# Centering the last sequence's output on ScalarE, and finishing the last group in two halves

## The chip, the cores and the metric

One core of one Trainium2 chip runs the whole program. The metric is the device time of one execution in microseconds (us). Each core has five engines with their own instruction queues: TensorE (PE in the profile, its weight loads PEld), VectorE (DVE), ScalarE (ACT), GpSimd (POOL) and SyncE (SP), which here issues most transfers. Instructions of different engines run side by side and wait for each other through semaphores; within one engine they start in the order in which they were issued.

## The reference

The input is x, 4 sequences of 2048 tokens with 256 features in float32. The reference applies two layers, each with a residual and a layer norm without gain:

```python
x = layernorm(x + attn(x))       # attn: q, k, v from small MLPs with gelu; scores = tril(q k^T) / scale;
                                 # out = layernorm(scores v) * ln_w + ln_b   (no softmax)
x = layernorm(x + ffn(x))        # ffn: soft mixture of experts over 256 slots (16 experts x 16)
```

In the second layer, tokens are normalized and compared with 256 slot vectors. One softmax (over tokens' logits for a slot) makes the slots' inputs, each expert's MLP turns them into slot outputs `so`, and a second softmax (over the slots, for a token) combines these into the token's output. The kernel's last step for a token is then `layernorm(row + combine @ so)`: the mean and variance over 256 features, the inverse root, and (value - mean) * root.

## The kernel before

The tokens are cut into 16 groups of 512 (W), four per sequence (NG); a group is four chunks (G) of 128 tokens, one token per partition. A group's tokens lie in a buffer `row`, 128 partitions x 4 chunks x 257 values. Eight such buffers exist.

The order of the work is not written out by hand. Functions such as `attend`, `norms`, `back`, `softmaxes`, `slots` and `finish` declare steps with `plan.step(engine, length, emit, reads, writes)`, and `plan.run` is a list scheduler: it repeatedly takes the step that can begin earliest by the given lengths, with ties by rank, and emits its instructions. So a changed length, engine or dependence can move other steps on each engine's queue, and buffers with several places are given out in that order.

`finish(t, so)` ends group t. For each chunk c, TensorE multiplies the combining weights `ct` by the slot outputs `so_t` into a PSUM bank (`ps_at`, three banks; L1265). The product, scaled by a per-token factor `sc`, is added to `row` in one of two ways:

- on VectorE, one instruction from PSUM (L1289);
- in the last sequence (`part` is set), for chunks 1 and 3: ScalarE scales the product from PSUM into a buffer `xn` (L1274), and POOL adds that to `row` (L1281).

`means` then takes VectorE's statistics of the chunk (L532) and their mean and variance (L533) into `mv`. When all four chunks are there, VectorE forms variance + eps (`ve`, L1299), POOL raises it to the power -0.5 (`inv_root`, L521), and `center_on` centers the chunks: first VectorE computes nm = -mean * root for the group (L557), which a ScalarE centering takes as its bias. Then each chunk is centered on the engine that a list names: ScalarE (`Identity` with scale and bias, L567), or VectorE or POOL (`tensor_scalar` with two operations, L573). The list is this:

```python
["ACT"] * G if part is None else
("DVE", "ACT", "POOL", "DVE") if t == ngroups - 1 else ("ACT", "POOL") * 2,
```

SyncE stores the group (L1313), the last group (15) in two halves of two chunks, all others in one transfer of 512 KB.

The finish steps of the sequence before the last (groups 8 to 11) are ranked late (`late = 100`), so they come near the end, just ahead of groups 12 to 15. As built, the eight stores at the end are those of groups 8, 9, 10, 12, 11, 13, 14 and the two halves of 15.

Of the kernel before, what the change touches and what calls it, by code (L numbers as in the profile page):

```python
# [9 lines left out]
AF = mybir.ActivationFunctionType  # L10
ALU = mybir.AluOpType
# [3 lines left out]
P = 128  # L15
G = 4
LAST = 2
W = G * P
LN_EPS = 1e-5
# [164 lines left out]
def _act(n, pointers=0):  # L184
    return 0.16 + 0.00083 * n + 0.093 * pointers
# [6 lines left out]
def _pool(n):  # L192
    return 0.1 + 0.0022 * n


def _pe(n):
    return max(0.22, 0.00168 * n)
# [6 lines left out]
def kernel(  # L204
# [13 lines left out]
    nc = tc.nc  # L218
    B, T, C = x.shape
# [4 lines left out]
    EH = ES // P  # L224
# [11 lines left out]
    ngroups = B * NG  # L236
    plan = Plan()
# [165 lines left out]
    for n, after in (  # L403
# [29 lines left out]
        out=mask,  # L433
        in_=ones,
# [13 lines left out]
    so_t = const.tile([P, EH, C], F32, name="so")  # L448
# [53 lines left out]
    def turn_in(bounce, dst):  # L502
        def emit():
            for a in range(P // 32):
                rows_ = slice(32 * a, 32 * (a + 1))
                nc.sync.dma_start(
                    out=dst[rows_].rearrange("c k (n r) -> c k n r", r=32),
                    in_=bounce[:, :, rows_].rearrange("k (n c) r -> c k n r", c=32),
                )

        plan.step("SP", 2.2, emit, [bounce], [dst])
        plan.step(
            "DVE", _dve(KC * W), lambda: nc.vector.transpose(out=dst.place, in_=dst.place),
            [], [dst],
        )

    def inv_root(v, n):
        r = plan.buffer("root")

        def emit():  # L520
            nc.gpsimd.tensor_tensor(  # L521
                r[:, :n], v[:, :n], nhalf.to_broadcast([P, n]), ALU.pow
            )

        plan.step("POOL", 1.04, emit, [v], [r])
        return r

    def means(src, st, mv, c, access):


        def emit():
            nc.vector.bn_stats(st[:, c, :], access())  # L532
            nc.vector.bn_aggr(mv[:, c, :], st[:, c, :])  # L533

        plan.step("DVE", 0.6, emit, [src], [(st, [c]), (mv, [c])])

    def variances(mv):
        return mv[:, :, 1:2].rearrange("p c o -> p (c o)")
# [10 lines left out]

            plan.step("DVE", 0.42, emit, [mv, r], [(dst, [c])])  # L550

    def center_on(dst, mv, r, engines):

        nm = plan.buffer("root")
        plan.step(
            "DVE", 0.17,
            lambda: nc.vector.scalar_tensor_tensor(  # L557
                nm.place, mv[:, :, 0:1].rearrange("p c o -> p (c o)"), -1.0, r.place,
                ALU.mult, ALU.mult,
            ),  # L560
            [mv, r], [nm],
        )
        for c in range(G):

            def emit(c=c):
                if engines[c] == "ACT":
                    nc.scalar.activation(  # L567
                        dst[:, c, :C], dst[:, c, :C], AF.Identity,
                        bias=nm[:, c : c + 1], scale=r[:, c : c + 1],
                    )  # L570
                else:
                    eng = nc.vector if engines[c] == "DVE" else nc.gpsimd
                    eng.tensor_scalar(  # L573
                        dst[:, c, :C], dst[:, c, :C], mv[:, c, 0:1], r[:, c : c + 1],
                        ALU.subtract, ALU.mult,
                    )

            length = {"ACT": _act(C, 2), "DVE": 0.42, "POOL": _pool(C)}[engines[c]]
            plan.step(
                engines[c], length, emit, [nm if engines[c] == "ACT" else mv, r], [(dst, [c])]  # L580
            )

    def spread(col, name):
# [317 lines left out]
    def norms(t):  # L901
# [17 lines left out]
        for c in range(G):  # L919
# [16 lines left out]
        )  # L936
        rr = inv_root(w2, G)
        center_on(row, mv2, rr, ("DVE", "ACT") * 2)
        plan.step(
            "DVE", 0.17,  # L940
# [139 lines left out]
    def by_blocks(t):  # L1080

        return t < ngroups - LAST
# [164 lines left out]
    def finish(t, so):  # L1247

        b, g = divmod(t, NG)
        row, _, sq, sc = n_tiles.pop(t)
        ct = c_tiles.pop(t)
        if by_blocks(t):
            bounce, ct = ct, plan.buffer("ct", EH)
            turn_in(bounce, ct)
        st, mv = plan.buffer("st", G), plan.buffer("mv", G)

        part = plan.buffer("xn", G) if t >= ngroups - NG else None
        for c in range(G):  # L1260
            pc = plan.buffer("ps_at")

            def emit(c=c, pc=pc):
                for h in range(EH):
                    nc.tensor.matmul(  # L1265
                        pc[:, :C], ct[:, h, c * P : (c + 1) * P], so_t[:, h, :],
                        start=(h == 0), stop=(h == EH - 1),
                    )

            plan.step("PE", EH * _pe(C), emit, [ct, so], [pc])  # L1270
            if part and c % 2:

                def emit(c=c, pc=pc):
                    nc.scalar.activation(  # L1274
                        part[:, c, :], pc[:, :C], AF.Copy, scale=sc[:, c : c + 1]
                    )

                plan.step("ACT", _act(C, 1), emit, [pc, sc], [(part, [c])])

                def emit(c=c):  # L1280
                    nc.gpsimd.tensor_tensor(  # L1281
                        row[:, c, :C], row[:, c, :C], part[:, c, :], ALU.add
                    )

                plan.step("POOL", _pool(C), emit, [(part, [c])], [(row, [c])])
            else:

                def emit(c=c, pc=pc):
                    nc.vector.scalar_tensor_tensor(  # L1289
                        row[:, c, :C], pc[:, :C], sc[:, c : c + 1], row[:, c, :C],  # L1290
                        ALU.mult, ALU.add,
                    )

                plan.step("DVE", 0.48, emit, [pc, sc], [(row, [c])])
            means((row, [c]), st, mv, c, lambda c=c: row[:, c, :C])
        ve = plan.buffer("ve")

        def emit():
            nc.vector.scalar_tensor_tensor(  # L1299
                ve.place, sq.place, LN_EPS, variances(mv), ALU.mult, ALU.add  # L1300
            )

        plan.step("DVE", 0.17, emit, [mv, sq], [ve])
        center_on(
            row, mv, inv_root(ve, G),
            ["ACT"] * G if part is None else
            ("DVE", "ACT", "POOL", "DVE") if t == ngroups - 1 else ("ACT", "POOL") * 2,
        )
        for c0 in range(0, G, G // 2) if t == ngroups - 1 else (0,):
            cs = slice(c0, c0 + (G // 2 if t == ngroups - 1 else G))  # L1310

            def emit(cs=cs):
                nc.sync.dma_start(  # L1313
                    out=out[b, g * W + cs.start * P : g * W + cs.stop * P, :].rearrange(
                        "(c p) d -> p c d", p=P
                    ),
                    in_=row[:, cs, :C],
                )

            plan.step("SP", 0.5, emit, [(row, list(range(cs.start, cs.stop)))], [])  # L1320


    plan.begin(-2.0)
# [8 lines left out]
    for t in range(ngroups):  # L1332
        plan.begin(t)
        attend(t)
        plan.begin(t + 0.7)
        norms(t)
        plan.begin(t + 0.8)
        load_x(t + 2)
        plan.begin(t + 1.2)
        back(t)  # L1340
        if t % NG == NG - 1:
            b = t // NG
            plan.begin(t + 1.5)
            softmaxes(b)


            late = 100.0 if b == B - 2 else 0.0
            plan.begin(t + 1.8 + late)
            so = slots(b)
            for i in range(NG):  # L1350
                plan.begin(t + 2.2 + 0.3 * i + late)
                finish(t - NG + 1 + i, so)
# [44 lines left out]
```

## Time and profile before

| | |
|---|---|
| Time, median of 3 runs | 691.25 us (691.01 to 691.26) |
| The profiled execution's own time | 689.66 us |
| Its span | 687.9 us, granted TensorE clock 0.993 |
| Busy in the span: PE, DVE, ACT, POOL | 660.1, 510.6, 252.3, 261.8 us |
| POOL centerings (L573) | 7, mean 1248 ns |
| ScalarE centerings (L567) | 87, mean 591 ns |
| VectorE centerings (L573) | 34, mean 411 ns |
| Roots on POOL (L521, 128x4) | 48, mean 1019 ns |
| Last matmuls of the program (L1265) | 660.83 to 674.91 us |
| Issues of the last five stores | 674.27, 676.42, 681.98, 683.80, 684.43 us |

The span is the time between the first and last instruction that the hardware profiler saw; the time of an execution also has what lies around it, 1.8 us in the profiled one. "x48 | 48.9, 1019" in a row of groups means 48 instructions that were busy for 48.9 us in total, 1019 ns each; what follows is idle time of the engine just before them and what ended it. Busy shares average over the whole program. At the end, when TensorE has stopped, other engines set the time, so the last 25 us are read by themselves.

### The profile page before, as it was taken

How to read it: one execution, taken by the hardware profiler on the slowest of the kernel's cores; microseconds unless marked ns; L12 is line 12 of the kernel's file. 1: busy time of each engine (PE TensorE's matmuls, PEld its weight loads, DVE VectorE, ACT ScalarE, POOL GpSimd, SP SyncE). 2: the span in 40 equal slices, each digit the busy share in tenths (PEclk: the TensorE clock that was granted, in tenths of full speed). 3: DMA queues.
4: the chain of work that ended last, by engine and by line, in shares of the span. 5: the costliest groups of instructions: out<-in, count | busy, mean ns of one | idle time of the engine just before them, and what ended most of it. 6: DMA issues, size and time to landing. Idle time of an engine off the chain costs nothing.

```text
span 687.9 us, 9055 instructions
## 1 busy us (share of the span) xinstructions
PE 660.1 (96%) x2974; PEld 502.9 (73%) x2974; DVE 510.6 (74%) x1316; ACT 252.3 (37%) x521; POOL 261.8 (38%) x255
## 2 busy tenths in 40 slices
PE   6999999999999999899999999999999999998982
PEld 4758767686868877768677886868676877877871
DVE  1438877968887588968797489998796897768394
ACT  3120335234154226241526125541526444415253
POOL 4260440232346017241418213543415545045247
PEclk9999999999999999999999999999999999999997
DMA  8793177556645146685655364775574316100044
GB/s 244 190 215 63 38 148 143 103 92 122 123 86 98 45 78 186 156 162 103 129 93 92 62 115 130 161 177 117 98 137 79 61 31 92 31 1 1 31 93 152
DMA packets 302462, 73.61 MB, mean 107 GB/s; under 512 B 240016, under 2 KB 302224, under 8 KB 302416
## 3 DMA queue, kind: packets, MB, share of 16 engines
q1 hardware_dynamic: 301312, 71.98, 50.0%
q10 hardware_dynamic: 960, 0.80, 0.4%
q8 instruction: 23, 0.38, 0.2%
q0 software_dynamic: 144, 0.26, 0.1%
q14 instruction: 23, 0.19, 0.1%
HBM read 42.61 MB, written 30.41 MB: 106 GB/s over the span
## 4 chain that ended last, share of the span: by engine, by line
PE 80%; DVE 9%; POOL 4%; DMA 3%; issue 1%; SPq 1%; ACT 1%; POOLq 0%; ACTq 0%; DVEq 0%
PE mm L714 21%; PE mm L1020 7%; PE mm L764 7%; PE at L816 7%; PE at L1142 6%; PE mm L737 6%; PE at L1265 6%; PE at L851 6%; PE at L789 4%; PE at L855 3%; PE at L859 3%; DVE st L532 2%; DMA both_sb<-in_W2q_dram 1%; DVE a_t L892 1%; POOL row L573 1%; POOL root L521 1%
## 5 line engine op out<-in xcount | busy, mean ns | idle before, releaser
L724 ACT ACTIVATE hid<-mm,cols_sb 128x512 f32<-128x512 f32 x96 | 65.1, 685 | 186.9 <-PE mm L714 173.9
L521 POOL TENSOR_TENSOR root<-ve,nhalf 128x4 f32<-128x4 f32 x48 | 48.9, 1019 | 202.0 <-DVE ve L915 76.8
L567 ACT ACTIVATE row<-row,root,root 128x256 f32<-128x256 f32 x87 | 46.5, 591 | 68.6 <-DVE root L557 68.4
L851 PE MATMUL at<-state,hid 128*128 128x256 f32 x240 | 61.8, 380 | 0.0
L737 PE MATMUL mm<-both_sb,hid 128*128 128x257 f32 x256 | 60.8, 381 | 0.9 <-DVE kt L747 0.7
L764 PE MATMUL mm<-W2v_sb,hid 128*128 128x256 f32 x256 | 59.0, 380 | 2.5 <-DVE lg L1030 2.0
L714 PE MATMUL mm<-xT,W1q_sb 128*128 128x512 f32 x128 | 60.7, 604 | 0.3 <-DVE xT L455 0.3
L1053 ACT ACTIVATE xn<-lg,nrm 128x256 f32<-128x256 f32 x64 | 32.0, 500 | 76.4 <-DVE lg L1030 76.3
L1265 PE MATMUL at<-so,ct 128*128 128x256 f32 x256 | 57.9, 380 | 1.8 <-DVE so L1242 1.8
L816 PE MATMUL at<-vt,kt 128*128 128x256 f32 x240 | 58.9, 379 | 0.0
L714 PE MATMUL mm<-xT,W1v_sb 128*128 128x512 f32 x128 | 58.5, 592 | 0.0
L1020 PE MATMUL mm<-mu_sb,xnT 128*128 128x256 f32 x256 | 58.1, 379 | 0.2 <-DVE kt L747 0.2
L714 PE MATMUL mm<-xT,W1k_sb 128*128 128x512 f32 x128 | 58.2, 592 | 0.0
L1142 PE MATMUL at<-row,lg 128*128 128x257 f32 x256 | 56.9, 380 | 0.0
L532 DVE BATCH_NORM_STATS2 st<-row 128x6 f32<-128x256 f32 x128 | 53.6, 419 | 4.0 <-POOL row L1281 1.9
L737 PEld LDWEIGHTS mm<-both_sb,hid 128*128 128x128 f32 x256 | 47.7, 190 | 12.0 <-issue 3.5
L764 PEld LDWEIGHTS mm<-W2v_sb,hid 128*128 128x128 f32 x256 | 48.2, 190 | 10.1 <-DVE lg L1030 2.4
L1265 PEld LDWEIGHTS at<-so,ct 128*128 128x128 f32 x256 | 48.1, 190 | 9.7 <-DVE so L1242 2.2
L1020 PEld LDWEIGHTS mm<-mu_sb,xnT 128*128 128x128 f32 x256 | 48.3, 190 | 8.7 <-issue 1.2
L1142 PEld LDWEIGHTS at<-row,lg 128*128 128x128 f32 x256 | 48.4, 189 | 7.4 <-issue 0.3
L851 PEld LDWEIGHTS at<-state,hid 128*128 128x128 f32 x240 | 45.4, 190 | 9.2 <-issue 2.6
L816 PEld LDWEIGHTS at<-vt,kt 128*128 128x128 f32 x240 | 45.3, 190 | 8.1 <-issue 1.2
(126 smaller groups left out, 1160.5 us busy)
## 6 DMA issues: line engine op xcount, KB each, us to landing
bounce<-xn SPq DMA_DIRECT2D x28, 512.0 KB, 3.2
row<-in_x_dram SPq DMA_DIRECT2D x16, 512.0 KB, 5.2
out_dram<-row SPq DMA_DIRECT2D x15, 512.0 KB, 2.9
xT<-in_x_dram SPq DMA_DIRECT2D x112, 64.0 KB, 2.4
bounce<-kt SPq DMA_DIRECT2D x28, 256.0 KB, 2.8
kT<-bounce SPq DMA_DIRECT2D x56, 128.0 KB, 2.9
xnT<-bounce SPq DMA_DIRECT2D x56, 128.0 KB, 3.6
ct<-bounce SPq DMA_DIRECT2D x56, 128.0 KB, 3.6
```

Source lines behind the costliest of these rows:

```text
L521: nc.gpsimd.tensor_tensor(r[:, :n], v[:, :n], nhalf.to_broadcast([P, n]), ALU.pow)
L532: nc.vector.bn_stats(st[:, c, :], access())
L567: nc.scalar.activation(dst[:, c, :C], dst[:, c, :C], AF.Identity, bias=nm[:, c : c + 1], scale=r[:, c : c + 1],)
L714: nc.tensor.matmul(ph.place, wa[f"W1{n}"][:, k, m * P : (m + 1) * P], xT[:, k, :], start=(k == 0), stop=(k == KC - 1),)
L724: nc.scalar.activation(hid[n][:, m, :], ph.place, AF.Gelu, bias=cols_sb[:, 4 * i + m : 4 * i + m + 1],)
L737: nc.tensor.matmul(pk[:, : C + 1], hid["k"][:, k, c * P : (c + 1) * P], wqk_sb[:, k, :], start=(k == 0), stop=(k == KC - 1),)
L764: nc.tensor.matmul(pv[:, j * C : (j + 1) * C], hid["v"][:, k, (c0 + j) * P : (c0 + j + 1) * P], wa["W2v"][:, k, :], start=(k == 0), stop=( ...
L816: nc.tensor.matmul(pds[:, m * C : (m + 1) * C], kt[:, c, m * P : (m + 1) * P], vt[:, c, :], start=True, stop=True,)
L851: nc.tensor.matmul(po[:, :C], qT[:, k, toks[c]], s[:, k, :], start=(k == 0), stop=False,)
L1020: nc.tensor.matmul(pl[:, j * ES : (j + 1) * ES], xnT[:, k, (c0 + j) * P : (c0 + j + 1) * P], mu_sb[:, k, :], start=(k == 0), stop=(k == KC ...
L1142: nc.tensor.matmul(psi[:, : C + 1], lg[:, c, h * P : (h + 1) * P], row[:, c, :], start=(i == 0 and c == 0), stop=(i == NG - 1 and c == G - 1),
L1265: nc.tensor.matmul(pc[:, :C], ct[:, h, c * P : (c + 1) * P], so_t[:, h, :], start=(h == 0), stop=(h == EH - 1),)
```

## The change

`center_on` gets a first chunk `c0` and a list of engines, one for each chunk from there on; it knows only ScalarE and VectorE. In `finish`, groups 12 to 14 now have all four chunks centered by ScalarE. Group 15 runs the whole ending (evict, statistics, variance, root, nm, centering, store) for chunks 0 and 1, and then for chunks 2 and 3, with the first of each pair centered by VectorE and the second by ScalarE. In group 15 the chunks that go through ScalarE and POOL's addition are now 0 and 2, not 1 and 3. The code for one chunk's product has moved into a function `combine`. The planner's length for a ScalarE centering is 0.55 in place of `_act(C, 2)`, which is 0.56.

```diff
-    def center_on(dst, mv, r, engines):
+    def center_on(dst, mv, r, engines, c0=0):
+        n = len(engines)
         nm = plan.buffer("root")
         plan.step(
             "DVE", 0.17,
             lambda: nc.vector.scalar_tensor_tensor(
-                nm.place, mv[:, :, 0:1].rearrange("p c o -> p (c o)"), -1.0, r.place,
-                ALU.mult, ALU.mult,
+                nm[:, :n], mv[:, c0 : c0 + n, 0:1].rearrange("p c o -> p (c o)"), -1.0,
+                r[:, :n], ALU.mult, ALU.mult,
             ),
-            [mv, r], [nm],
+            [(mv, list(range(c0, c0 + n))), r], [nm],
         )
-        for c in range(G):
+        for i, engine in enumerate(engines):
+            c = c0 + i
...
-                    eng = nc.vector if engines[c] == "DVE" else nc.gpsimd
-                    eng.tensor_scalar(
-                        dst[:, c, :C], dst[:, c, :C], mv[:, c, 0:1], r[:, c : c + 1],
+                    nc.vector.tensor_scalar(
+                        dst[:, c, :C], dst[:, c, :C], mv[:, c, 0:1], r[:, i : i + 1],
                         ALU.subtract, ALU.mult,
                     )
...
         part = plan.buffer("xn", G) if t >= ngroups - NG else None
-        for c in range(G):
-            pc = plan.buffer("ps_at")
...
-            if part and c % 2:
...
-        center_on(
-            row, mv, inv_root(ve, G),
-            ["ACT"] * G if part is None else
-            ("DVE", "ACT", "POOL", "DVE") if t == ngroups - 1 else ("ACT", "POOL") * 2,
-        )
-        for c0 in range(0, G, G // 2) if t == ngroups - 1 else (0,):
...
+        last = t == ngroups - 1
+        n = G // 2 if last else G
+        for c0 in range(0, G, n):
+            cs = list(range(c0, c0 + n))
+            for c in cs:
+                combine(c, row, ct, so, sc, part if part and (c + last) % 2 else None)
+                means((row, [c]), st, mv, c, lambda c=c: row[:, c, :C])
+            ve = plan.buffer("ve")
+            def emit(c0=c0, ve=ve):
+                nc.vector.scalar_tensor_tensor(
+                    ve[:, :n], sq[:, c0 : c0 + n], LN_EPS, variances(mv)[:, c0 : c0 + n],
+                    ALU.mult, ALU.add,
+                )
+            plan.step("DVE", 0.17, emit, [(mv, cs), sq], [ve])
+            center_on(row, mv, inv_root(ve, n), ("DVE", "ACT") if last else ("ACT",) * G, c0)
+            def emit(c0=c0):
+                nc.sync.dma_start(
+                    out=out[b, g * W + c0 * P : g * W + (c0 + n) * P, :].rearrange(
+                        "(c p) d -> p c d", p=P
+                    ),
+                    in_=row[:, c0 : c0 + n, :C],
+                )
+            plan.step("SP", 0.5, emit, [(row, cs)], [])
+
+    def combine(c, row, ct, so, sc, part):
+        pc = plan.buffer("ps_at")
...
+        plan.step("PE", EH * _pe(C), emit, [ct, so], [pc])
+        if part:
...
+                lambda: nc.scalar.activation(
+                    part[:, c, :], pc[:, :C], AF.Copy, scale=sc[:, c : c + 1]
+                ),
...
+                lambda: nc.gpsimd.tensor_tensor(
+                    row[:, c, :C], row[:, c, :C], part[:, c, :], ALU.add
+                ),
...
+            return
...
+            lambda: nc.vector.scalar_tensor_tensor(
+                row[:, c, :C], pc[:, :C], sc[:, c : c + 1], row[:, c, :C],
+                ALU.mult, ALU.add,
+            ),
```

## The prediction

> **What bounds it now.** I read the page first, then a table by stretch, then the chain that ended last. TensorE is busy for 96% of the span, so only what delays TensorE, or what comes after its last matmul, can move the end.
>
> ```profile
> span 687.9 us, 9055 instructions
> PE 660.1 (96%) x2974; PEld 502.9 (73%) x2974; DVE 510.6 (74%) x1316; ACT 252.3 (37%) x521; POOL 261.8 (38%) x255
> ```
>
> The built orders of the two kernels agree on TensorE in every row. On the other engines they part only after POOL's root of group 12, which starts at 667.68 us. So the change lives in the last 20 us. A table of stretches (busy us and count per engine, then clock, DMA share, GB/s):
>
> ```profile
> 676.30:682.00 5.70, 0.00 (x0) 0.00 (x0) 2.43 (x9) 1.09 (x2) 5.49 (x8) 0.73 0.33 114
> 682.00:687.90 5.90, 0.00 (x0) 0.00 (x0) 0.89 (x3) 0.60 (x1) 2.29 (x2) 0.50 0.51 178
> 682.90:684.40 1.50, 0.00 (x0) 0.00 (x0) 0.89 (x3) 0.60 (x1) 1.40 (x2) 0.50 0.94 339
> 684.70:686.20 1.50, 0.00 (x0) 0.00 (x0) 0.00 (x0) 0.00 (x0) 0.00 (x0) 0.50 0.99 336
> ```
>
> After TensorE's end (674.9) POOL is busy 5.49 of 5.70 us and ScalarE 1.09: POOL is the engine of the tail. In the last two rows DMA engines are 94 and 99% busy: a store in flight fills them, at 336 to 339 GB/s. The chain that ended last, in order of time (start, us, what):
>
> ```profile
> 667.68 1.03 POOL root L521
> 668.81 2.44 POOL row L573 x2
> ...
> 672.81 1.04 POOL root L521
> 673.94 2.46 POOL row L573 x2
> 676.40 0.61 POOL row L1281
> ...
> 678.37 1.04 POOL root L521
> 679.50 2.45 POOL row L573 x2
> 681.95 0.99 POOL root L521
> 682.99 1.42 POOLq L1390
> ```
>
> POOL's centerings (L573) are on the chain in three groups, and group 15's root at 681.95 waits behind group 14's centering. Its own input was ready at 679.57. Meanwhile ScalarE, which holds the other centerings, stands still before group 14 and again before group 15:
>
> ```profile
> 675.38 0.59 ACT L567 ACTIVATE row<-row,root,root 128x256 f32<-128x256 f32 x1
> 679.67 1.09 ACT L567 ACTIVATE row<-row,root,root 128x256 f32<-128x256 f32 x2 [3.71 <-DVE root L557]
> 683.17 0.60 ACT L567 ACTIVATE row<-row,root,root 128x256 f32<-128x256 f32 x1 [2.41 <-DVE root L557]
> ```
>
> The last POOL centering ends at 684.40. The last store is issued at 684.43 and lands 2.3 us later at 686.7; closing the program takes the span to 687.9, 1.15 more. Prices, grouped by form (count, then total us, mean ns):
>
> ```profile
> L521 POOL TENSOR_TENSOR root<-ve,nhalf 128x4 f32<-128x4 f32 x48 | 48.9, 1019 | 202.0 <-DVE ve L915 76.8 <-DVE ve L941 56.7 <-DVE ve L1299 43.4
> L567 ACT ACTIVATE row<-row,root,root 128x256 f32<-128x256 f32 x87 | 46.5, 591 | 68.6 <-DVE root L557 68.4
> L573 DVE TENSOR_SCALAR row<-row,mv,root 128x256 f32<-128x256 f32 x34 | 12.7, 411 | 0.0
> L573 POOL TENSOR_SCALAR row<-row,mv,root 128x256 f32<-128x256 f32 x7 | 8.7, 1248 | 0.4
> L521 POOL TENSOR_TENSOR root<-cm,nhalf 128x2 f32<-128x2 f32 x1 | 0.7, 723 | 8.9 <-DVE nscale L626 8.9
> ```
>
> The stores from 660 us on:
>
> ```profile
> DMA to landing us min/median/max: 2.2/2.9/3.0
> ```
>
> **What the Trainium skill says.** "ScalarE: Activation LUTs", section "What ACT_TABLE_LOAD costs", prices an ACTIVATE with a pointer bias at 280 ns + 0.833 per element, 93 more for a second pointer, and lets neighbours overlap by 93. For 256 elements that is 586 ns, and 493 from start to start. The trace agrees: 591 ns, and the four centerings of group 10 start at 661.21, 661.71, 662.20, 662.70. "SBUF — State Buffer", "Who interferes with whom", says that VectorE instructions with two SBUF inputs contend with GpSimd's reads, and that ScalarE waits on nobody at those ports. The trace agrees: the variance step L1299 took 581 ns at 677.71 beside POOL's additions, 164 at 679.40. "DMA: Bandwidth & Descriptors", "Issuing engines are not separate DMA queues", says all transfers share the same 16 engines; the 0.99 share above agrees.
>
> **The change, part by part.** Removed: seven POOL centerings, 7 x 1.25 = 8.7 us (two each in groups 12 to 14, one in 15). Added: seven ScalarE centerings, 7 x 0.49 = 3.45 us of its queue. Group 15 gets a second variance step and a second nm step (L557) on VectorE, about 0.16 us each, and two roots of 128x2 (723 ns, the one row of that shape) in place of one of 128x4: 1.45 against 1.02. Group 15's chunks trade evictors: 0 and 2 now go through ScalarE and POOL's addition, 1 and 3 through VectorE. VectorE's two centerings stay in number, and so do the stores.
>
> Now the order as built, with the starts of before as long as nothing moved. ScalarE: eviction of group 14's chunk 1 at 669.83; three centerings of group 12 from 670.20; eviction at 671.67 (as before, TensorE paces it); fourth centering 672.03; eviction of group 15's chunk 0 at 672.52 (its matmul ends 672.32). At 672.89 one centering of group 11, at 673.38 one of group 13. The eviction of chunk 2 follows its matmul (674.05), at 674.09. Then three of group 13 from 674.46 (an eviction holds the queue 0.37), three of group 11 from 675.93, and the queue is free for group 14 at 677.41.
>
> Does anything feed it late? POOL first: add of group 13 at 668.70, add of group 14's chunk 1 at 670.38 to 671.06, root of group 13 at 671.34 to 672.36, so its nm is there by 672.55, 0.8 before ScalarE asks. Group 11's nm is now queued behind four statistics pairs on VectorE, at 672.32 to 672.45 against 670.17 before; ScalarE asks at 672.89, so this delay costs nothing, with 0.44 in hand. VectorE then: eviction of group 15's chunk 1 at 673.22 (0.48); statistics of it and of group 14's last chunk at about 0.56 a pair, to 674.94; group 14's variance step at 674.97, which POOL's addition (674.64 to 675.30) holds to 675.30. POOL's root of group 14: 675.38 to 676.40. VectorE goes on: chunk 3's eviction 675.22, statistics, variance of the first half at 676.3, two more pairs, and only then group 14's nm at 677.48 to 677.61, though its root was ready at 676.40. So ScalarE waits 0.24 and starts group 14 at 677.65: four centerings, ended at 679.73. First half of group 15 at 679.62, second at 680.12, ended at 680.72. The half roots (676.5 to 677.25, 677.8 to 678.6) are 1.5 us or more ahead of that: splitting the root is hidden behind group 14's centerings on ScalarE; without that cover it would cost its 0.43.
>
> So compute ends at 680.7 rather than 684.4: 3.7 gained. But the stores bunch. Group 13 goes out at 676.1, group 11 at 677.5; each fills the DMA engines for 512 KB / 338 GB/s = 1.55 us. Group 14's store is issued at 679.76, and the halves at 680.25 and 680.76. Group 14 alone lands 2.9 later, at 682.66; the 512 KB of both halves queue behind it for 1.55 more: 684.2. Without the queue the last half would land at 680.76 + 2.3 = 683.1. Before, group 14 was issued 1.8 and 2.45 us ahead of the halves, and its data was out of the way; this is where 1.1 of the 3.7 goes. Closing adds 1.15: span 685.4, that is 2.5 less. The profiled execution took 689.66 and would take 687.2; the runs' median is 1.59 above it, and I carry the same 2.5 over: 691.25 - 2.5 = 688.75. About 0.2%, 1.4 us, is what a measurement can tell from no change.
>
> **Unknowns.** The 128x2 root on this data is bounded by 0.72 and 1.02; both are hidden. How two stores share the engines: between no delay (gain 3.6) and full serial drain (2.5). I take the drain, since the trace shows 0.94 to 0.99 busy for a single stream. The ScalarE walk could be late through nm steps blocked by POOL's additions, at most 0.7 for each of two.
>
> **Rivals.** *Drain free.* The halves' data slips between group 14's: last landing 683.1, span 684.3, time 687.6. For it: stores land in 2.2 at best. Against: the DMA share.
>
> *ScalarE starves.* The new head of its queue is a wait: group 11's or 13's centering now stands ahead of chunk 2's eviction, and group 14's waits on an nm that VectorE reaches late. Each blocked VectorE step moves everything behind it, and the group 14 store, one for one. Two blocks of 0.7 leave 2.5 - 1.4 = 1.1: 690.1, within 0.2%. For it: 0.58 for L1299 beside an addition. Against: slack of 0.44 and 0.8 at the first two places, and no additions are left after 675.3.
>
> *Slower.* The same wait at group 13's nm, but long: chunk 2's eviction, POOL's addition and the second half's variance stand behind it. From a delay of 0.8 on it eats the gain; at 3.3 nothing is left, and 4.7 makes it 692.7. The longest block of such a step in the trace is 2.13 us (L557 at 267.88, behind a 128x1024 POOL addition); the tail has only additions of 0.63 to 0.74. So this is remote.
>
> *Not doing what it says.* Excluded for the order: ScalarE has the centerings in the built program, and no table load is added.
>
> **Numbers.** Forecast with the drain 0.70; drain free 0.13; starved 0.12; slower 0.04, and 0.01 for noise of other kinds. Its own range is 688.0 to 689.5; with drain free and half of the starved case, 687.4 to 690.0. Faster 0.85 (nearly all of the first two and a little of the starved case), within 0.2% 0.11, slower 0.04.
>
> **What would show it.** Right: no POOL L573-like row in the tail; POOL idle from about 678.6; ScalarE near continuous from 669.8 to 680.7, with one short wait before group 14; the chain's end running through ScalarE centerings and then a DMA; the last half landing over 3 us after its issue. Wrong: a ScalarE wait of a microsecond before group 11 or 13, or the last store landing in 2.3.

## The result, and the profile after

The changed kernel took 688.86 us, the median of 9 runs (686.51 to 689.49); the kernel before, run beside it, took 691.01 (9 runs, 688.35 to 693.22). The ratio is 0.9964, with an interval of 0.9946 to 0.9983. The forecast was 688.75 us, in a range of 687.4 to 690.0.

The profiled execution seems to say otherwise: 689.35 us with a span of 687.6, hardly below the 689.66 and 687.9 of before. The page's head:

```profile
span 687.6 us, 9056 instructions
PE 661.8 (96%) x2974; PEld 503.9 (73%) x2974; DVE 511.0 (74%) x1318; ACT 255.6 (37%) x528; POOL 253.9 (37%) x249
```

ScalarE has 7 instructions more and POOL 6 fewer (seven centerings less, one root more), as declared. TensorE has the same 2974 matmuls and is busy for 661.8 us, where it was 660.1. So this execution lost time in TensorE that the change does not touch. The chain that ended last, in order of time (start, us, what):

```profile
654.78 4.95 DMA ct<-bounce
...
659.86 1.25 DVE ct L513
661.10 0.32 DVE so L1244
...
661.47 14.05 PE at L1298 x56
...
677.27 0.34 DVE ve L1273
677.62 0.39 DVE row L1322
678.01 0.34 DVE st L532
...
678.59 0.16 DVE ve L1273
...
679.65 0.18 DVE mv L533
679.83 0.06 DVE root L559
679.89 0.03 issue
679.91 1.58 ACT row L570 x3
681.50 0.49 ACTq L1397
681.99 0.98 ACT row L570 x2
```

From the last matmul on there is no POOL centering in it. VectorE's statistics run to the nm step of group 14 (L559, 679.83), and ScalarE's six centerings follow it without a break. Before that, the last phase's matmuls began at 661.47, behind a transfer, and ended at 677.23. In the kernel before they ran from 660.83 to 674.91. This part is 2.3 us later, and it lies ahead of the first instruction that the change moves. ScalarE's and POOL's timelines near the end:

```profile
676.41 0.47 ACT L1307 ACTIVATE xn<-at,sum 128x256 f32<-128x256 f32 x1
676.78 6.19 ACT L570 ACTIVATE row<-row,root,root 128x256 f32<-128x256 f32 x12
```

```profile
677.70 1.83 POOL L521 TENSOR_TENSOR root<-ve,nhalf 128x4 f32<-128x4 f32 x2
680.17 0.80 POOL L521 TENSOR_TENSOR root<-ve,nhalf 128x2 f32<-128x2 f32 x1 [0.64 <-DVE root L559]
```

Twelve centerings stand on ScalarE in one stretch, with a gap of only 0.09 us ahead of group 14; the waits of 3.71 and 2.41 us of before are gone. POOL ends with the second half's root.

To compare the kernels apart from TensorE, I use the *tail*: the end of the span less the end of the last matmul. It was 12.97 us before (687.88 - 674.91) and is 10.38 after (687.62 - 677.23): 2.59 us less. The medians differ by 2.2 us, and the interval of the ratio leaves 1.2 to 3.7, so the times and the tail agree; the profiled execution's 0.3 us does not, and the next part shows why.

### The profile page after: what moved, and what is told of

Same layout as the page of the kernel before. It is cut to its first block, busy times and chain, and to the rows that moved or that the text cites. A ratio compares the mean times of both kernels' runs of the same rounds, so it can differ in the third digit from the quotient of the medians.

```text
span 687.6 us, 9056 instructions
## 1 busy us (share of the span) xinstructions
PE 661.8 (96%) x2974; PEld 503.9 (73%) x2974; DVE 511.0 (74%) x1318; ACT 255.6 (37%) x528; POOL 253.9 (37%) x249
## 4 chain that ended last, share of the span: by engine, by line
PE 81%; DVE 9%; DMA 3%; POOL 2%; issue 1%; ACT 1%; SPq 1%; ACTq 0%; DVEq 0%; POOLq 0%
PE mm L716 21%; PE at L1298 8%; PE mm L766 7%; PE mm L1022 7%; PE at L818 7%; PE at L1144 6%; PE mm L739 6%; PE at L853 6%; PE at L791 4%; PE at L857 3%; PE at L861 3%; DVE st L532 2%; DVE a_t L894 1%; DMA both_sb<-in_W2q_dram 1%; DMA xnT<-bounce 1%
## 5 line engine op out<-in xcount | busy, mean ns | idle before, releaser
L521 POOL TENSOR_TENSOR root<-ve,nhalf 128x4 f32<-128x4 f32 (+1 forms) x49 | 49.6, 1012 | 202.9 <-DVE ve L917 77.0
L570 ACT ACTIVATE row<-row,root,root 128x256 f32<-128x256 f32 x94 | 49.7, 591 | 63.1 <-DVE root L559 62.9
L1298 PE MATMUL at<-so,ct 128*128 128x256 f32 x256 | 59.5, 388 | 2.4 <-DVE so L1244 2.4
```

The source lines that it names most:

```text
L521: nc.gpsimd.tensor_tensor(r[:, :n], v[:, :n], nhalf.to_broadcast([P, n]), ALU.pow)
L570: nc.scalar.activation(dst[:, c, :C], dst[:, c, :C], AF.Identity, bias=nm[:, i : i + 1], scale=r[:, i : i + 1],)
L1298: nc.tensor.matmul(pc[:, :C], ct[:, h, c * P : (c + 1) * P], so_t[:, h, :], start=(h == 0), stop=(h == EH - 1),)
```

## The experiments

### The changed kernel once more

> The changed kernel as it is, profiled once more. In its first profile the last matmul ended 2.32 us later than in the kernel before (677.23 against 674.91), with a gap of 2.42 us in TensorE before the last phase and TensorE's clock halved for 3.4 us after it. If this comes with the execution and not with the kernel, another execution can end its last matmul near 674.9 and the tail behind it is 10.4 again, so that its span is near 685.3. If it comes with the changed kernel, the last matmul ends near 677.2 again.

No edit. Its profiled execution took 687.07 us:

```profile
span 685.4 us, 9056 instructions
PE 660.5 (96%) x2974; PEld 502.9 (73%) x2974; DVE 510.9 (75%) x1318; ACT 255.4 (37%) x528; POOL 253.7 (37%) x249
```

The last matmul ended at 674.97, 0.06 from the kernel before; the tail was 10.38 again. So the 2.3 us came with the execution and not with the kernel. The median of 20 runs was 689.02 beside 691.33 of the kernel before (ratio 0.9968, 0.9953 to 0.9982).

Two things made up these 2.3 us in the first profile. The first was a late transfer. VectorE's timeline there has this row:

```profile
659.86 1.25 DVE L513 STREAM_TRANSPOSE ct<-ct 128x1024 f32<-128x1024 f32 x1 [0.67 <-DMA ct<-bounce]
```

The transposition waited 0.67 us for its load, and it stands ahead of the two additions that make `so`, for which TensorE waits. The last of SyncE's four issues of that load had taken 1.92 us; in the other profile none took over 0.57 and there was no wait. The second was the clock, in a table of stretches of the first profile (busy us and count of PE, PEld, DVE, ACT, POOL, then granted clock, DMA share, GB/s):

```profile
661.00:662.00 1.00, 0.53 (x2) 0.45 (x2) 1.00 (x5) 0.16 (x1) 0.00 (x0) 0.78 0.00 0
662.00:663.00 1.00, 1.00 (x4) 0.82 (x3) 0.93 (x5) 1.00 (x3) 0.00 (x0) 0.50 0.00 0
664.00:665.00 1.00, 1.00 (x4) 0.74 (x4) 0.67 (x4) 0.00 (x0) 0.00 (x0) 0.52 0.10 33
665.00:666.00 1.00, 1.00 (x6) 0.90 (x5) 0.00 (x0) 0.47 (x1) 0.27 (x1) 1.00 0.97 349
```

TensorE, back at work, did 4 matmuls per us rather than 6, at a clock of 0.50, from 661.56 to 664.97. At half the clock, half of these 3.41 us is lost, 1.7; with the 0.64 by which the phase began later this is the 2.3. More on this in the last section.

### One part alone: engines, or halves

> Only the engine change: the kernel before with groups 12 to 14 centered by ScalarE alone; group 15 keeps its four engines and its one root. 'Tail' is the span's end less the end of the last matmul (13.0 us before, 10.3 after). Theory (POOL's centerings were the tail): 10.7 us and a gain of about 2.2 us; a little less than the whole change, because the planner now puts group 11 behind group 15, so that a full store goes out last. Rival (the halves carry the gain): a tail of 12 us or more.

```diff
-            ("DVE", "ACT", "POOL", "DVE") if t == ngroups - 1 else ("ACT", "POOL") * 2,
+            ("DVE", "ACT", "POOL", "DVE") if t == ngroups - 1 else ("ACT",) * G,
```

The kernel before with this line: tail 10.74, median 688.87 of 20 runs beside 691.51 (ratio 0.9964, 0.9950 to 0.9979). Its chain at the end runs through ScalarE and no longer through POOL:

```profile
675.51 3.44 ACT row L567 x7
678.95 0.49 ACTq L1390
679.44 0.98 ACT row L567 x2
```

The edit also moves a store, as expected: a full one of 512 KB now goes out last, 5.90 after the last matmul, and lands at 9.59. So this tail is not quite the changed kernel's without the halves.

> Only the halves: group 15 as in the changed kernel, groups 12 to 14 centered by ScalarE and POOL in turn as before. Theory: POOL still ends group 14's centering about 7 us after the last matmul and both roots of group 15 stand behind it; tail 12.7 us, gain 0.2 us. Rival (the halves carry the gain): tail 11.5 us or less.

```diff
-            center_on(row, mv, inv_root(ve, n), ("DVE", "ACT") if last else ("ACT",) * G, c0)
+            center_on(row, mv, inv_root(ve, n), ("DVE", "ACT") if last else
+                ("ACT",) * G if part is None else ("ACT", "POOL") * 2, c0)
```

The changed kernel with this, and POOL allowed as an engine again: tail 12.66, median 691.20 of 20 runs beside 691.51 (0.9995, 0.9980 to 1.0009). Its chain still runs through POOL:

```profile
676.00 2.46 POOL row L576 x2
678.46 0.61 POOL row L1316
...
680.44 1.04 POOL root L521
681.48 0.09 issue
681.58 1.23 POOL row L576
682.80 1.20 POOLq L1399
684.00 1.36 POOL root L521 x2
```

Both half roots wait for group 14's centerings on POOL. So the six centerings of groups 12 to 14 carry the result: they alone take 2.23 us off the tail (12.97 - 10.74), the halves alone 0.31, and both together 2.59.

### What the second root costs

> The changed kernel with one variance step, one root and one nm for all four chunks of group 15; engines, evictors and stores as in the changed kernel. Theory (the split of the root is hidden behind group 14's centerings on ScalarE): tail 10.3 us, within 0.1. Rival (each half's own root lets it start earlier): tail 10.8 us or more.

```diff
-        n = G // 2 if last else G
+        n = G
...
-            center_on(row, mv, inv_root(ve, n), ("DVE", "ACT") if last else ("ACT",) * G, c0)
+            center_on(row, mv, inv_root(ve, n), ("DVE", "ACT") * 2 if last else ("ACT",) * G, c0)
+        for c0 in range(0, G, G // 2 if last else G):
+            n = G // 2 if last else G
```

Group 15 with one variance step, root and nm, still stored by halves: tail 10.21, median 688.34 (0.9954, 0.9940 to 0.9967; no difference from the changed kernel that these times can tell). The changed kernel's tails in three profiles are 10.38, 10.38 and 10.40 (the third with six more matmuls ahead of the last phase, further below), so 0.17 is more than their scatter. Group 14's store was issued 4.58 us after the last matmul rather than 4.78. What is gone ahead of it is the first half's variance step on VectorE, the row of 0.16 at 678.59 in the chain above: it stands ahead of group 14's nm. Splitting the root costs 0.17, on VectorE, not on POOL.

### The drain of the stores

> The changed kernel without the store of group 14; that quarter of the last sequence's output is left out. Theory (stores bunch, and the last half queues behind group 14's 512 KB): the last half lands 2.3 to 2.4 us after its issue in place of 3.4, tail 9.2 us. Rival (the landing is late for another reason, such as the first half): 3.4 us and 10.3 us stay.

```diff
-            plan.step("SP", 0.5, emit, [(row, cs)], [])
+            if t != ngroups - 2:
+                plan.step("SP", 0.5, emit, [(row, cs)], [])
```

Tail 9.38 (9.2 was expected), median 688.01 of 13 runs. The times from issue to landing of the last three stores, in the second profile of the changed kernel (group 14 and the halves) and in this run (group 11 and the halves):

```profile
DMA to landing us min/median/max: 2.9/3.2/3.4
DMA to landing us min/median/max: 2.2/2.4/2.9
```

The last half is the slowest of the first three, with 3.44 (3.43 in the first profile), and the middle one of the others, with 2.41: the queue behind group 14's store is worth 1.02 us. The issue was at 5.77 after the last matmul in one and 5.81 in the other, so no engine's work explains it. In the second profile of the changed kernel, the transfers from 678 to 686 us in 40 slices of 0.2 us look like this (busy tenths of the DMA engines, GB/s; the program ends with nine stores, of groups 8 to 15, and the last four fall in here):

```profile
DMA  9999999999100599999999999999700000000000
GB/s 364 282 328 379 379 364 364 374 358 348 62 0 0 184 358 343 343 333 343 353 343 302 374 348 343 333 348 353 231 10 0 0 0 0 0 0 0 0 0 0
```

Group 11's store is out at 680.1. From 680.6 to 683.9 one unbroken stream at some 340 GB/s carries group 14 and both halves: 1 MB. Both halves were issued by 680.8, while group 14's data was still under way, so their own issue times have no part in the stream's end.

### Bringing the stream forward

If the stream's start sets the end, group 14's store must go out earlier. Three edits try it.

> The changed kernel, with group 11's four centerings and its store planned ahead of those of groups 12 and 13, so that ScalarE does them earlier; the same work in all. It tells what group 14's start waits on. If it waits for its nm step on VectorE (which in the changed kernel ended 0.04 us before ScalarE's start of group 14), nothing changes at the end: a tail of 10.3, give or take 0.15. If it waits for ScalarE's backlog of groups 11 and 13, or if group 11's store stands in the way of group 14's, the tail is lower than 10.38 by 0.2 or more.

```diff
+            root = inv_root(ve, n)
+            was = plan.base, plan.count
+            if t == ngroups - NG - 1:
+                plan.begin(ngroups + 1.0)
-            center_on(row, mv, inv_root(ve, n), ("DVE", "ACT") if last else ("ACT",) * G, c0)
+            center_on(row, mv, root, ("DVE", "ACT") if last else ("ACT",) * G, c0)
+            plan.base, plan.count = was
```

Tail 10.20, median 688.02 (0.9963, 0.9951 to 0.9975). ScalarE now had all of group 11 behind it, and stood still for 1.38 us ahead of group 14:

```profile
681.88 3.06 ACT L570 ACTIVATE row<-row,root,root 128x256 f32<-128x256 f32 x6 [1.38 <-DVE root L559]
```

Yet group 14 started only 0.18 earlier (2.50 after the last matmul in place of 2.68), and its store went out at 4.60 in place of 4.78; the last half again took 3.42 to land. So it is VectorE's nm that group 14 waits for, as the chain said, and group 11's store was not in the way of the changed kernel's stream. The 0.18 came from VectorE too: in the order of this run, group 14's variance step stands behind an eviction and no longer beside a POOL addition, and took 0.15 us in place of 0.34.

> The changed kernel, with two of group 14's four centerings on VectorE instead of ScalarE; everything else as in the changed kernel. From the end of the last matmul to the end of the span the changed kernel took 10.38 us. If the walk of ScalarE sets the end and the stores queue behind it, ScalarE has 2 x 0.49 = 1.0 us less to do, group 14's store goes out about 1.0 earlier (3.8 after the last matmul in place of 4.78) and the halves with it, but group 11's store, issued at 2.6, then stands closer ahead of them: 0.3 of the 1.0 is given back and the tail is about 9.7. If the stores' drain alone sets the end, whatever the engines do, the tail stays at 10.4. If VectorE, which also has the statistics of group 15, becomes the engine that is late, the tail is above 10.4.

```diff
-            center_on(row, mv, inv_root(ve, n), ("DVE", "ACT") if last else ("ACT",) * G, c0)
+            center_on(row, mv, inv_root(ve, n), ("DVE", "ACT") if last else
+                ("DVE", "DVE", "ACT", "ACT") if t == ngroups - 2 else ("ACT",) * G, c0)
```

Tail 9.80 (9.7 expected), median 687.14 of 5 runs (0.9950, 0.9933 to 0.9966). Group 14's store at 3.80, as expected. But VectorE's two centerings now stand ahead of the second half's variance step, which starts 0.97 later than in the changed kernel. POOL's root waits 1.54 us for it, and VectorE then 0.81 for the root, here in their timelines:

```profile
682.71 0.69 POOL L521 TENSOR_TENSOR root<-ve,nhalf 128x2 f32<-128x2 f32 x1 [1.54 <-DVE ve L1273]
```

```profile
681.44 0.73 DVE L575 TENSOR_SCALAR row<-row,mv,root 128x256 f32<-128x256 f32 x2
...
682.48 0.15 DVE L1273 SCALAR_TENSOR_TENSOR ve<-re,mv 128x2 f32<-128x2 f32 x1
683.44 0.16 DVE L559 SCALAR_TENSOR_TENSOR root<-mv,root 128x2 f32<-128x2 f32 x1 [0.81 <-POOL root L521]
```

The last half's store is issued at 5.39, 1.1 behind the first half's (4.29) where it was 0.54. This costs little as long as the stream is longer: the last half still took 3.26 to land.

> Both of the two edits at once: group 11's centerings and store planned ahead, and two of group 14's centerings on VectorE. If the edit of group 14 gains 1.0 on the engines and gives part of it back to group 11's store, then here that store is out of the way and the tail is about 9.3 us, against 10.38 of the changed kernel and 12.97 of the kernel before; the median would be some 3.6 below the kernel before and 1 below the changed one. If group 11's store never stood in the way, the tail is that of the group 14 edit alone.

The edit is the two above in one. Tail 9.24 (9.3 expected), median 687.19 of 6 runs (0.9949, 0.9936 to 0.9962). Against the edit of group 14 alone, group 14's store and both halves go out 0.18 earlier (3.62, 4.11, 5.21), for the reason given above, and the last half lands 2.88 after its issue rather than 3.26. The two differences, 0.18 and 0.38, add up to the 0.56. So group 11's store, harmless to the changed kernel, is in the way once group 14's comes 1 us earlier.

> The kernel with group 11 planned ahead and group 14 shared with VectorE (tail 9.24 us), with group 14's store cut into two of 256 KB each, one behind each pair of centerings. If the drain of the last stores sets the end from group 14's store on, it now starts about 0.5 us earlier (group 14's first pair is ready 3.1 after the last matmul, its store went out at 3.6): the data of four pieces of 0.78 each follows from there, and the tail is about 8.9. The floor is the last half alone: issued at 5.2, 2.3 to its landing and 1.15 to close, 8.7. If the drain isn't what sets the end, the tail stays at 9.2.

On top of the two edits:

```diff
+            if t == ngroups - 2:
+                for c in range(0, G, 2):
+                    def emit(c=c):
+                        nc.sync.dma_start(
+                            out=out[b, g * W + c * P : g * W + (c + 2) * P, :].rearrange(
+                                "(c p) d -> p c d", p=P
+                            ),
+                            in_=row[:, c : c + 2, :C],
+                        )
+                    plan.step("SP", 0.5, emit, [(row, [c, c + 1])], [])
+                continue
             plan.step("SP", 0.5, emit, [(row, cs)], [])
```

Tail 8.70, median 686.86 of 15 runs (0.9937, 0.9917 to 0.9957). The two new stores went out at 3.15 and 3.63. The last half, issued at 5.21 as in the kernel before this edit, landed 2.40 later; it took 2.41 in the run without group 14's store. So the queue is gone, the floor of 8.7 is met, and ScalarE's last centering, behind VectorE's late variance, sets the end again:

```profile
681.74 1.58 ACT L570 ACTIVATE row<-row,root,root 128x256 f32<-128x256 f32 x3 [1.39 <-DVE root L559]
683.82 0.60 ACT L570 ACTIVATE row<-row,root,root 128x256 f32<-128x256 f32 x1 [0.49 <-DVE root L559]
```

### TensorE's clock

> The changed kernel with six matmuls more, 128x256 each, whose result nobody reads; they stand on TensorE just ahead of the last phase's first matmul, which waits 1.75 us for its operand on VectorE. They shorten no wait: the last matmul ends where it did and the tail is 10.4. If TensorE's clock is halved for 3.4 us because TensorE was busy for less than half of a 3.4 us window, it is not halved at 661 to 667 us any more, in any execution; about half of the executions then save 1.7 us, and the median is some 0.8 below the changed kernel's 688.9 to 689.0. If the halving has another cause, the executions spread as before and the median stays.

Matmuls whose result nobody reads, called idle matmuls here, fill TensorE's wait ahead of the last phase. (`combine` also gets `t` as an argument, not shown.)

```diff
...
         def emit():
+            if t == ngroups - NG and c == 0:
+                for k in range(6):
+                    nc.tensor.matmul(
+                        pc[:, C : 2 * C], ident, w2_sb[:, k, :], start=True, stop=True
+                    )
             for h in range(EH):
```

Tail 10.40, and the clock full from its first record at 8.7 us to the last matmul. But six were too many, as TensorE's timeline shows:

```profile
659.78 2.86 PE L1299 MATMUL at<-w_sb,ident 128*128 128x256 f32 x12
662.47 3.83 PE L1303 MATMUL at<-so,ct 128*128 128x256 f32 x17
```

Each of the six ran as two instructions, and the twelve took 2.86 us by the timeline, from 659.78 to 662.64. The first of the two additions that make `so` ended at 661.65; in the kernel before, the last phase's first matmul began within 0.1 us of the end of that addition. From the end of the phase before to the last matmul it took 16.60 us, against 15.83 with the idle wait and a full clock, and 17.52 with the idle wait and a halved one. So an execution with the idle matmuls pays 0.77, and one that would have been halved saves the 1.69, 0.92 net. The median was 688.13 of 22 runs beside 691.20. That is the number expected, but the ratio, 0.9966 (0.9953 to 0.9980), can't be told from the changed kernel's 0.9968.

> The kernel with group 11 planned ahead, group 14 shared with VectorE and its store cut in two, with the six idle matmuls as well. Tail 8.9 us, no halved clock at 661 to 667 us; a median of about 686.6, some 2.3 below the changed kernel and 4.6 below the kernel before. If the halving has another cause, about 0.8 more.

The same edit on the kernel with group 14's store in two. Tail 8.72, no halved clock in its profile before the end, 16.60 us again; median 686.66 of 17 runs (0.9944, 0.9929 to 0.9959). All executions lay between 685.26 and 688.46. The median can't be told from that without the idle matmuls (0.9937, 0.9917 to 0.9957).

> The same as the run before it with group 14's store cut in two and idle matmuls, but with three of them in the program in place of six. Six ran as twelve instructions and took 2.6 us, longer than the wait of 1.75 that they were to fill, and put the last phase back by 0.77 us. Three fill 1.3 of the 1.75: the time from the end of the phase before to the last matmul is 15.83 us again (16.60 with six, 17.52 with none and a halved clock), the clock is not halved there, the tail is 8.7, and the median is some 0.8 below the 686.66 of six: about 685.9. If three leave the clock to be halved, the median is 686.7 or more and single executions reach 689.

```diff
-                for k in range(6):
+                for k in range(3):
```

Now TensorE's timeline has a short wait left:

```profile
661.19 1.56 PE L1317 MATMUL at<-w_sb,ident 128*128 128x256 f32 x6
663.40 1.35 PE L1321 MATMUL at<-so,ct 128*128 128x256 f32 x5 [0.65 <-DVE so L1244]
```

Tail 8.70, clock full from there to the last matmul. The stretch took 16.22 us, not 15.83: the load of `ct` was late by 0.39 in this execution, with one issue of 2.10 us on SyncE, as in the first profile of the changed kernel. The median was 685.44 of 6 runs (684.03 to 687.89) beside 690.46: ratio 0.9911, 0.9884 to 0.9938. By its ratio this version beats both kernels, the one before by 5 us; from the one with six idle matmuls, six runs can't tell it. The profiled execution was the slowest of the six: its clock was halved once, after a wait near 290 us that no idle matmul fills.

## Why the prediction was right

The prediction followed each engine's queue step by step to the end; this is called its walk here. Counted from the last matmul (predicted 674.91), each step can be compared with the first profile and with the second, which had no halved clock up to the last matmul.

| | predicted | first profile | second |
|---|---|---|---|
| ScalarE starts group 14 | 2.74 | 2.68 | 2.68 |
| Store of group 14, first half, second half | 4.85, 5.34, 5.85 | 4.78, 5.27, 5.81 | 4.78, 5.28, 5.81 |
| POOL's end | 3.7 | 3.74 | 3.74 |
| Last landing | 9.3 | 9.24 | 9.25 |
| Last landing to the end | 1.15 | 1.14 | 1.14 |
| Tail | 10.5 | 10.38 | 10.38 |
| Span | 685.4 | 687.6 | 685.4 |
| Time of the profiled execution | 687.2 | 689.35 | 687.07 |

- **POOL is the engine of the tail.** Shown: with the centerings of groups 12 to 14 back on POOL the tail is 12.66; with them away and nothing else, 10.74.
- **Group 14 starts when VectorE has reached its nm.** Shown by the early group 11, with which ScalarE stood still for 1.38 us and still had to wait for the nm. In the changed kernel this wait was 0.09 rather than 0.24.
- **The stores bunch and give back 1.1.** The last store was issued 3.71 earlier than before (5.81 against 9.52 after the last matmul; 3.7 predicted), but the tail is only 2.59 shorter. The mechanism holds, and the queue behind group 14's store was 1.02, by the run without it. "Drain free", with a landing in 2.3, fell. The note of the Trainium skill that all transfers share 16 engines ("DMA: Bandwidth & Descriptors", "Issuing engines are not separate DMA queues") agrees with the unbroken stream of 1 MB at some 340 GB/s, though here SyncE issued all of it.
- **The split root is hidden.** Only the roots are hidden. The step that mattered was priced beside them, "a second variance step ... on VectorE, about 0.16 us": it stands in the walk to group 14's nm, and the run with one root is 0.17 shorter. This term was in the walk's sum, but the prediction did not name it as a cost of the split.
- **ScalarE starves / slower.** Neither happened: VectorE's variance step of group 14 was held to 0.34 us beside a POOL addition (L1273 at 677.27), as assumed, and from the first centering of group 12 on ScalarE never waited more than 0.15. One step was not foreseen: group 13's nm, expected to end 2.36 before the last matmul's end, took 0.60 beside a POOL addition and ended at 1.96. It used up half of the 0.8 that the prediction had in hand there, so nothing came of it.
- **The same 2.5 is carried to the median.** It held (2.15 beside the first nine runs, 2.31 in the later set), but not for a reason that the prediction gave. It took the 1.59 us between the profiled execution and the median as a constant. By the last section, executions with a halved clock, which costs 1.7 each time, probably make up most of it; the profiled one of before had none up to its last matmul. This is not shown, for the other executions have a mean clock and no trace. The waits that go with a halved clock stand at the same places in both kernels, which would explain why the difference stayed. That the median came within 0.11 us of the forecast is luck, as the interval leaves 1.2 to 3.7 us for the gain.

## What to carry to other kernels

When a change acts only behind the last matmul, measure the span from that matmul on: it repeated to 0.02 us here while whole executions of one kernel differed by 5. Here, moving work from the engine of the tail paid until the stores bunched; from there the end was the start of the last unbroken stream plus its bytes over its rate, and an earlier first store of that stream was what helped (cutting group 14's store in two gained 0.54), until an engine was the last again. Walk a tail engine by engine in the built order, and include the small steps of the engine that merely feeds: a variance step of 0.16 us showed as 0.17 here.

## What the runs showed of the hardware that was not expected

A single kernel's executions spread over some 5 us (686.03 to 691.40 in 20 runs of the changed kernel), and the spread goes with the granted TensorE clock: the seven with a mean clock of 0.996 took 687.12 on average, the four with 0.994 took 688.43, the five with 0.991 took 691.05; the other four, at 0.992 and 0.993, lay between.

The profiles show how. Every change of the clock before the end falls on a grid of 3.413 us that starts at a different point of each execution (8.7 to 12.0 us after the span's start): the records lie 191, 196, 197, 82, 108, 113, 5 or 1 of these units apart. A halved clock lasted one unit in every case and came right after a unit in which TensorE had been busy for less than half, worked out from its instructions in the traces:

```
TensorE's busy share of one unit     next unit's clock, all 14 profiles, up to the last matmul
0.24 to 0.44                         halved, 9 of 9
0.45 to 0.50                         halved, 3 of 7
0.53 and more                        full, all
```

The two waits that matter are one near 288 us (one piece of 1.96 to 2.58 us in eleven profiles, two pieces of under 1 in three) and one at 660, of 1.75 us in nine of the eleven profiles without idle matmuls. Both are shorter than a unit. A wait of 1.75 leaves a share of 0.49 if it falls wholly inside a unit, and more if the grid cuts it. So whether it costs 1.7 us more depends on where the grid happens to lie. At the border, 0.45 to 0.50, these profiles do not tell what decides. The Trainium skill says ("TensorE: Matmul & The Clock Gate", "What's actually happening") that the clock is set by a free-running window of 3413 ns, which agrees with the grid. Its rule of thumb in "HAM oscillation — how this bites in real kernels", no idle gaps of more than about 3.4 us, is too generous here: in three of the five units that held a wait of 1.75 us whole, it was enough.

In all three profiles with idle matmuls in the wait at 660 us the clock stayed full there, and in 5 of the 11 without them it was halved. That fits but three profiles alone would not prove it. Why single issues of SyncE's loads of `ct` took 1.9 and 2.1 us in two executions, against 0.3 to 0.8 in the others, stays open. In both executions the first piece of that load, issued in the usual time, was late as well: it landed 4.05 and 4.15 us after its issue, against 2.6 to 2.9.
